# Turning sums over states on TensorE in two halves of 64 channels: a selective-scan block on one Trainium2 core

## The chip, the cores and the metric

The kernel runs on one core of a Trainium2 chip. The metric is device time in microseconds (us) of one execution. The kernel before took 2935.89 us (median of two runs, 2935.25 and 2936.52). The profile shown here is of one further execution of the same kernel, which took 2932.42 us, of which 2930.6 us are the span of its instructions. All times of engines, spacings and waits below are of that execution.

## What is computed

The input is x of 8 x 2048 x 512. A layer norm is followed by a selective scan (state space model with 16 states per channel), added back to x; a second layer norm is followed by a matmul with int8 quantised rows, added back as well. The part that the change touches is the sum over states and the skip term:

```python
deltaA = jnp.exp(jnp.einsum('bld,dn->bldn', delta, A))
deltaB_u = jnp.einsum('bld,bln,bld->bldn', delta, Bm, x)
def step(h, inp):
    dA_t, dBu_t, C_t = inp
    h = dA_t * h + dBu_t
    y = jnp.einsum('bdn,bn->bd', h, C_t)
    return (h, y)
...
y = ys.transpose(1, 0, 2) + x * D
...
x = x + _L0_attn_ref(_layernorm(x, axis=-1), ...)
x = x + _L0_ffn_ref(_layernorm(x, axis=-1), ...)
```

## The kernel before

**Tiling.** The 16384 rows are cut into 32 chunks of 512 time steps; four consecutive chunks are one sequence. In a chunk, the scan runs with channels on the partitions and time along the free axis. The 512 channels are four blocks d of 128, the 512 steps four blocks i of 128. One pair (state n, block d) is a unit; a chunk has 16 x 4 = 64 units, called slots, and there are 2048 units u in all.

**One slot.** ScalarE makes da = exp(delta * A) (`exp_unit`, L673). ScalarE also scales x by B for one block i of a coming state (`bt_piece`, L689). TensorE turns that to channels by time, 4 transposes of 128 x 128 into one PSUM bank pb (`b_pe`, L712). For the states 1, 4, 9, 13 (`DIAG_STATES`) it multiplies by a diagonal matrix of B instead (L703; every fp32 matmul that is no transpose runs as two passes, so 8 matmuls in the trace). VectorE runs the scan over 512 steps (`scan`, L721). Once per state, GpSimd multiplies the four finished blocks of h by C (`c_mult`, L749). TensorE turns hc back to time by channels and sums over states in PSUM in the same step: `y_pe` (L763) is 4 transposes of 128 x 128 for one time block i, into the bank y_i, with `start` only on the first of 16 states. `skip_pe` (L778) adds x * D to the same bank, 4 matmuls (8 passes) with `diag_d`, in the slots `SKIP_AT` = 45, 47, 49 and 51. The last state of the last chunk is turned in `finish` (L799).

**Order.** All instructions are kept in program order on each engine. The main loop goes through the units u and issues, in this order: `c_mult` (when d = 0), `exp_unit`, `bt_piece`, `b_pe(u + 2)`, `scan(u)`, `y_pe(u - 11)`, and then the steps that two tables place in this slot. `PREP_AT` holds the preparation of the next chunk (layer norm, transposes, projections), `POST_AT` (`LATE_AT` for the last two) the second half of the previous chunk: residual add, layer norm, quantisation, the int8 matmul and the store. So TensorE runs two units ahead of VectorE's scan, and the turn of hc runs 11 units behind. The last `y_pe` of a chunk for i = 0, 1, 2, 3 come in slots 7, 8, 9, 10 of the next chunk; the residual adds that read them (L546, VectorE) in slots 8, 10, 12, 13; the first `y_pe` of the next chunk, which write the same banks, in slots 11, 12, 13, 14.

**PSUM.** Eight banks: four for y (tags y0 to y3), three for pb (one pool, `bufs=3`), one for all else (`misc`).

Of the kernel before, what the change touches and what calls it, by code (L numbers as in the profile page):

```python
# [9 lines left out]
F32 = mybir.dt.float32  # L10
# [4 lines left out]
ALU = mybir.AluOpType  # L15
AX = mybir.AxisListType

P = 128
T = 512
LN_EPS = 1e-05  # L20
Q_EPS = 1e-06
# [23 lines left out]

POST_AT = dict(
    load=(0, 6),
    residual=(8, 10, 12, 13),
    stats=(15, 18, 20, 22),
    aggregate=(16, 19, 21, 23),  # L50
    rstd=23,
# [13 lines left out]

LATE_AT = dict(
    load=(0, 6),
    residual=(8, 10, 12, 13),
    stats=(15, 18, 20, 22),
    aggregate=(16, 19, 21, 23),  # L70
    rstd=23,
# [19 lines left out]
def kernel(  # L91
# [13 lines left out]
    nc = tc.nc  # L105

    B, L, DM = x.shape
    N = a_log.shape[1]
# [3 lines left out]
    ND = DM // P  # L112
# [16 lines left out]
    small = ctx.enter_context(tc.tile_pool(name="small", bufs=6))  # L129
    dram = ctx.enter_context(tc.tile_pool(name="dram", bufs=2, space=bass.MemoryType.DRAM))  # L130
    diagd = ctx.enter_context(tc.tile_pool(name="diagd", bufs=1, space=bass.MemoryType.DRAM))
    ps_y = ctx.enter_context(tc.tile_pool(name="ps_y", bufs=1, space=bass.MemoryType.PSUM))
# [3 lines left out]
    pin = tc.keep_in_program_order  # L136
# [15 lines left out]
    ident = const.tile([P, P], F32, name="ident")  # L152
# [31 lines left out]
    diag_d = const.tile([P, ND, P], F32, name="diag_d")  # L184
# [33 lines left out]
    xn_t, delta, b_t = {}, {}, {}  # L218
# [3 lines left out]
    das, pbs, bts, hs, hcs, ys = {}, {}, {}, {}, {}, {}  # L222
# [158 lines left out]
    def prep_first(second):  # L381
# [3 lines left out]
        mv = small.tile([P, NT, 2], F32, tag=f"mv{NT}", name="mv_0")  # L385
# [9 lines left out]
        pts, pps = {}, {}  # L395
# [49 lines left out]
        def dt(i):  # L445
            for d in range(ND):
                if i == 0:
                    pps[d] = ps_y.tile([P, T], F32, tag=f"y{d}", name=f"pdt_0_{d}")
                pin(
                    nc.tensor.matmul(  # L450
                        pps[d][:, ts(i, P)],
                        lhsT=dtproj_sb[:, ts(d, P)],
                        rhs=xp[:, ts(i, P)],
                        start=True,
                        stop=True,
                    )
                )
# [71 lines left out]
        pin(nc.sync.dma_start(out=bias_b, in_=bias.partition_broadcast(P)))  # L529
        zero_diagonals(1)  # L530

    def post(k):

        key = f"f{k}"
# [7 lines left out]
        def x1_of(i):  # L542
            return x1[k, i // 2][:, i % 2, :]

        def residual(i):
            pin(nc.vector.tensor_tensor(x1_of(i), ys.pop((k, i)), x1_of(i), ALU.add))  # L546

        def norm(i):
            if i == 0:
# [201 lines left out]

    def y_pe(s, i):

        if s < 0 or s >= LAST - 1:
            return
        k, n = divmod(s, N)
        if n == 0:
            y = ps_y.tile([P, DM], F32, tag=f"y{i}", name=f"y_{k}_{i}")
            ys[k, i] = y
        y = ys[k, i]  # L760
        for d in range(ND):
            pin(
                nc.tensor.matmul(  # L763
                    y[:, ts(d, P)],
                    lhsT=hcs[s][:, d, ts(i, P)],
                    rhs=ident,
                    is_transpose=True,
                    start=(n == 0 and d == 0),
                    stop=(n == N - 1 and d == ND - 1),
                    skip_group_check=True,  # L770
                )
            )

    def skip_pe(k, i):

        for d in range(ND):
            pin(
                nc.tensor.matmul(  # L778
                    ys[k, i][:, ts(d, P)],
                    lhsT=xn_t[k][:, d, ts(i, P)],  # L780
                    rhs=diag_d[:, d, :],
                    start=False,
                    stop=False,
                    skip_group_check=True,
                )
            )

    def finish():


        k, s = NCHUNK - 1, LAST - 1
        h = hs.pop(s)
        hc = work.tile([P, ND, T], F32, tag="hc", bufs=3, name=f"hc_{k}_{N - 1}")
        c = cts[s // 2][:, (N - 1) % 2, :]
        for d in range(ND):
            pin(nc.vector.tensor_tensor(hc[:, d, :], h[:, d, :], c, ALU.mult))
            for i in range(NT):
                pin(
                    nc.tensor.matmul(  # L799
                        ys[k, i][:, ts(d, P)],  # L800
                        lhsT=hc[:, d, ts(i, P)],
                        rhs=ident,
                        is_transpose=True,
                        start=False,
                        stop=(d == ND - 1),
                        skip_group_check=True,
                    )
                )
        mv = small.tile([P, NT, 2], F32, tag=f"mv{NT}", name="mv_last")
        am = small.tile([P, NT], F32, tag="am", name="am_last")  # L810
        xs = small.tile([P, NT], F32, tag="xs", name="xs_last")
        rs = small.tile([P, NT], F32, tag="rs", name="rs_last")
        ve = small.tile([P, NT], F32, tag="ve", name="ve_last")
        rstd = small.tile([P, NT], F32, tag="rstd", name="rstd_last")
        nmr = small.tile([P, NT], F32, tag="nmr", name="nmr_last")

        z_all = work.tile([P, NT, DM], F32, tag="z", bufs=1, name="z_last")

        def x1_of(i):
            return x1[k, i // 2][:, i % 2, :]  # L820

        def measure(i):
            one = slice(i, i + 1)
            t = x1_of(i)
            pin(nc.vector.tensor_tensor(t, ys.pop((k, i)), t, ALU.add))
            st = small.tile([P, 6], F32, tag="st", name=f"st_last_{i}")
            pin(nc.vector.bn_stats(st, t))
            pin(nc.vector.bn_aggr(mv[:, i, :], st))
            pin(nc.vector.tensor_scalar(ve[:, one], mv[:, i, 1:2], LN_EPS, None, ALU.add))
            pin(nc.gpsimd.tensor_tensor(rstd[:, one], ve[:, one], nhalf[:, one], ALU.pow))  # L830

        def norm(i):
            one = slice(i, i + 1)
            pin(
                nc.vector.tensor_scalar(
                    nmr[:, one], mv[:, i, 0:1], -1.0, rstd[:, one], ALU.mult, ALU.mult
                )
            )
            pin(
                nc.scalar.activation(  # L840
                    z_all[:, i, :], x1_of(i), AF.Identity, bias=nmr[:, one], scale=rstd[:, one]
                )
            )

        def quantise(i):
            one = slice(i, i + 1)
            z = z_all[:, i, :]
            pin(
                nc.vector.tensor_reduce(
                    am[:, one], z, AX.X, ALU.max, apply_absolute_value=True  # L850
                )
            )
            pin(
                nc.vector.tensor_scalar(
                    xs[:, one], am[:, one], Q_EPS, 1.0 / 127.0, ALU.max, ALU.mult
                )
            )
            pin(nc.vector.reciprocal(rs[:, one], xs[:, one]))
            pin(nc.scalar.activation(z, z, AF.Copy, bias=ROUND, scale=rs[:, one]))
            pin(nc.gpsimd.tensor_tensor(x1_of(i), x1_of(i), bias_b, ALU.add))  # L860
            pz = ps_b.tile([P, T], F32, tag="b", name=f"pz_last_{i}")
            for d in range(ND):
                pin(nc.tensor.transpose(pz[:, ts(d, P)], z[:, ts(d, P)], ident))
            qt = work.tile([P, ND, P], BF16, tag="qT", name=f"qT_last_{i}")
            pin(
                nc.scalar.activation(
                    qt, pz.rearrange("p (d t) -> p d t", t=P), AF.Copy, bias=-ROUND
                )
            )
            po = ps_y.tile([P, T], F32, tag=f"y{i}", name=f"po_last_{i}")  # L870
            for d in range(ND):
                pin(
                    nc.tensor.matmul(
                        po, lhsT=qt[:, d, :], rhs=wq_sb[:, d, :], start=(d == 0), stop=(d == ND - 1)
                    )
                )
            return po

        def output(i, po):
            o = z_all[:, i, :]  # L880
            pin(
                nc.vector.scalar_tensor_tensor(
                    o, po, xs[:, i : i + 1], ws_b, ALU.mult, ALU.mult
                )
            )
            adder = nc.vector if i == NT - 1 else nc.gpsimd
            pin(adder.tensor_tensor(o, o, x1_of(i), ALU.add))
            pin(nc.sync.dma_start(out=of[ds(k * T + i * P, P), :], in_=o))

        pos = {}  # L890
        measure(0)
        measure(1)
        norm(0)
        measure(2)
        norm(1)
        pos[0] = quantise(0)
        measure(3)
        norm(2)
        pos[1] = quantise(1)
        norm(3)  # L900
        pos[2] = quantise(2)
        output(0, pos[0])
        pos[3] = quantise(3)
        for i in range(1, NT):
            output(i, pos[i])
# [93 lines left out]
```

## Time and profile before

| | |
|---|---|
| Median of two runs | 2935.89 us |
| The profiled execution, its span | 2932.42 us, 2930.6 us |
| TensorE clock granted | 0.997 of full, over the span |
| First scan starts, last scan starts | 29.4 us, 2901.6 us |
| DMA | 276.46 MB, mean 94 GB/s; largest queue 30.5% of 16 engines' span |
| GpSimd, hc (L749) | 511 x 4566 ns |
| ScalarE, exp (L673) and x * B (L689) | 2048 x 714 ns and 1532 x 712 ns |
| VectorE, residual add (L546) | 124 x 665 ns |

How to read it: PE stands for TensorE's matmuls and PEld for its weight loads, which run beside the matmuls; DVE is VectorE, ACT ScalarE, POOL GpSimd. A transpose is a matmul whose loaded weight is the data (`lhsT`) and whose moving operand is the identity. The duration of a PE row is from start to end of one matmul, and matmuls are pipelined: the rate is read from the distance of starts. In a row of the timeline that holds several instructions (x4), this distance is (length of the row - duration of one) / (count - 1).

### The profile page before, as it was taken

The page shows a single profiled execution, that of the slowest core. Times are in us where ns is not written, and L with a number is a line of the kernel's source. Part 1 is how long each engine was busy: PE and PEld are TensorE (multiplying, and loading weights), DVE is VectorE, ACT ScalarE, POOL GpSimd, SP SyncE. Part 2 cuts the span into 40 slices and gives each one's busy share as a digit, 9 for nine tenths or more (in the row PEclk, how much of TensorE's full clock was granted, in tenths as well). Part 3 has the DMA queues.
Part 4 walks back from the last instruction along what each step waited for, and adds up shares of the span by engine and source line. Part 5 has one row for each costly group of instructions (what it writes and reads, how often), then busy time and mean ns, then how long its engine had stood idle before and what let it go on. Part 6 is the DMA issues. An engine that isn't in the chain of part 4 may idle for free.

```text
span 2930.6 us, 57694 instructions
## 1 busy us (share of the span) xinstructions
PE 2771.6 (95%) x22132; PEld 2461.9 (84%) x22226; DVE 2875.5 (98%) x3077; ACT 2785.3 (95%) x4477; POOL 2791.0 (95%) x1335
## 2 busy tenths in 40 slices
PE   8999999999999999999999999999999999999987
PEld 6888888888888888888888888888888888888886
DVE  6999999999999999999999999999999999999998
ACT  7999999999999999999999999999999999999994
POOL 6899999999999999999999999999999999999997
PEclk9999999999999999999999999999999999999999
DMA  4232332322333323323233332233232232323221
GB/s 139 84 102 72 96 109 95 109 77 88 98 106 98 97 68 106 107 92 107 80 86 103 96 107 81 84 105 99 98 102 77 91 109 95 109 77 88 85 90 62
DMA packets 179989, 276.46 MB, mean 94 GB/s; under 512 B 79169, under 2 KB 79681, under 8 KB 179713
## 3 DMA queue, kind: packets, MB, share of 16 engines
q1 hardware_dynamic: 177520, 272.41, 30.5%
q8 instruction: 174, 2.85, 0.4%
q14 instruction: 103, 0.84, 0.1%
q10 hardware_dynamic: 2192, 0.36, 0.1%
HBM read 235.77 MB, written 36.96 MB: 93 GB/s over the span
## 4 chain that ended last, share of the span: by engine, by line
PE 48%; ACT 30%; DVE 12%; issue 6%; POOL 3%; DMA 1%; ACTq 0%; DVEq 0%; SPq 0%
PE y L763 13%; ACT da L673 12%; PE pb L712 11%; PE pb L703 10%; ACT bT L689 9%; DVE h L721 8%; PE pxp L294 4%; PE po L611 3%; POOL hc L749 3%; PE y L778 2%; PE pdt L333 2%; ACT delta L343 2%; ACT z L552 1%; ACT L673 1%; ACT L343 1%
## 5 line engine op out<-in xcount | busy, mean ns | idle before, releaser
L749 POOL TENSOR_TENSOR hc<-h,c 128x2048 f32<-128x2048 f32 x511 | 2330.9, 4566 | 26.8 <-DVE mv_f L232 11.5
L721 DVE TENSOR_TENSOR_SCAN h<-da,state,pb 128x512 f32<-128x512 f32 x1536 | 1868.7, 1258 | 8.7 <-PE pb L703 3.4
L673 ACT ACTIVATE da<-delta,a_neg 128x512 f32<-128x512 f32 x2048 | 1417.0, 714 | 6.4 <-DVE h L721 5.9
L763 PE MATMUL y<-ident,hc 128*128 128x128 f32 x8176 | 1226.4, 273 | 0.3 <-POOL hc L749 0.3
L689 ACT ACTIVATE bT<-x,BT 128x512 f32<-128x512 f32 x1532 | 1090.4, 712 | 0.0
L712 PE MATMUL pb<-ident,bT 128*128 128x128 f32 x6128 | 948.6, 277 | 83.5 <-DVE h L721 64.2
L712 PEld LDWEIGHTS pb<-ident,bT 128*128 128x128 f32 x6128 | 705.3, 141 | 315.1 <-DVE h L721 132.1
L763 PEld LDWEIGHTS y<-ident,hc 128*128 128x128 f32 x8176 | 957.3, 141 | 1.3 <-POOL hc L749 0.5
L721 DVE TENSOR_TENSOR_SCAN h<-da,pb 128x512 f32<-128x512 f32 x512 | 593.7, 1200 | 17.8 <-PE pb L712 12.2
L703 PE MATMUL pb<-dg,x 128*128 128x128 f32 x4128 | 552.3, 277 | 24.3 <-DVE h L721 21.7
L703 PEld LDWEIGHTS pb<-dg,x 128*128 128x128 f32 x4128 | 506.3, 192 | 59.0 <-DVE h L721 37.1
L564 POOL TENSOR_TENSOR x<-x,bias_b 128x1024 f32<-128x1024 f32 x62 | 147.5, 2379 | 2.5
L632 POOL TENSOR_TENSOR z<-z,x 128x1024 f32<-128x1024 f32 x62 | 147.5, 2379 | 0.0
L333 PE MATMUL pdt<-xp,dtproj_sb 128*128 128x512 f32 x248 | 130.1, 606 | 17.8 <-ACT delta L343 17.8
L778 PE MATMUL y<-diag_d,xnT 128*128 128x128 f32 x1024 | 135.2, 275 | 0.0
L611 PE MATMUL po<-wq_sb,qT 128*128 128x512 bf16 x403 | 122.3, 379 | 8.3 <-ACT qT L600 3.2
L294 PE MATMUL pxp<-xnT,xproj_sb 128*96 128x512 f32 x248 | 126.7, 592 | 0.0
L778 PEld LDWEIGHTS y<-diag_d,xnT 128*128 128x128 f32 x1024 | 124.4, 192 | 0.0
L343 ACT ACTIVATE delta<-pdt,dtb_sb 128x512 f32<-128x512 f32 x124 | 85.0, 685 | 37.2 <-PE pdt L333 36.8
L288 ACT COPY xnT<-pxn 128x512 f32<-128x512 f32 x124 | 72.6, 585 | 34.0 <-PE pxn L282 31.9
L270 ACT ACTIVATE x<-x,nmr_a,rstd_a 128x512 f32<-128x512 f32 x124 | 100.8, 813 | 0.0
L552 ACT ACTIVATE z<-x,nmr_f,rstd_f 128x512 f32<-128x512 f32 x124 | 99.4, 803 | 0.0
(100 smaller groups left out, 1660.0 us busy)
## 6 DMA issues: line engine op xcount, KB each, us to landing
c<-bc SPq DMA_DIRECT2D x256, 512.0 KB, 4.0
x<-in_x_dram SPq DMA_DIRECT2D x64, 512.0 KB, 5.2
dg<-dg SPq DMA_DIRECT2D x127, 256.0 KB, 4.7
x<-in_x_dram SPq DMA_DIRECT2D x31, 1024.0 KB, 7.9
out_dram<-z SPq DMA_DIRECT2D x62, 512.0 KB, 4.8
dg<-zeros SPq DMA_DIRECT2D x8, 256.0 KB, 6.0
dg<-BT SPq DMA_DIRECT2D x128, 2.0 KB, 3.7
x<-in_x_dram SPq DMA_DIRECT2D x4, 256.0 KB, 3.9
```

The costliest lines, as they stand in the source:

```text
L294: nc.tensor.matmul(st["pp"][:E], lhsT=xproj_sb[:, d, :], rhs=xn_t[k][:, d, :], start=(d == 0), stop=(d == ND - 1),)
L333: nc.tensor.matmul(pd, lhsT=dtproj_sb[:, ts(d, P)], rhs=xp, start=True, stop=True)
L343: nc.scalar.activation(delta[k][:, d, :], st.pop(("pd", d)), AF.Softplus, bias=dtb_sb[:, d : d + 1])
L611: nc.tensor.matmul(po, lhsT=qt[:, d, :], rhs=wq_sb[:, d, :], start=(d == 0), stop=(d == ND - 1))
L673: pin(nc.scalar.activation(t, delta[k][:, d, :], AF.Exp, scale=a_neg[:, d, n : n + 1]))
L689: nc.scalar.activation(bts[s][:, i, :], xn[k][:, i, :], AF.Copy, scale=b_t[k][:, i, n : n + 1])
L703: nc.tensor.matmul(pb[:, ts(i, P)], lhsT=xn[k][:, i, ts(d, P)], rhs=bts[s][:, i, :], start=True, stop=True,)
L712: pin(nc.tensor.transpose(pb[:, ts(i, P)], bts[s][:, i, ts(d, P)], ident))
L721: nc.vector.tensor_tensor_scan(hs[s][:, d, :], das.pop(u), pbs.pop(u), 0.0 if k % CPB == 0 else state[n][:, d : d + 1], ALU.mult, ALU.add,)
L749: pin(nc.gpsimd.tensor_tensor(hc, h, c.unsqueeze(1).to_broadcast([P, ND, T]), ALU.mult))
L763: nc.tensor.matmul(y[:, ts(d, P)], lhsT=hcs[s][:, d, ts(i, P)], rhs=ident, is_transpose=True, start=(n == 0 and d == 0), stop=(n == N - 1 ...
L778: nc.tensor.matmul(ys[k, i][:, ts(d, P)], lhsT=xn_t[k][:, d, ts(i, P)], rhs=diag_d[:, d, :], start=False, stop=False, skip_group_check=True,)
```

## The change

Each transpose of `y_pe`, each transpose of `finish` and each matmul of `skip_pe` becomes two, one for channels 0 to 63 and one for channels 64 to 127 of the block, one after the other. A half has 64 contracted rows (partitions 0 to 63 or 64 to 127 of the data and of the identity or `diag_d`), still 128 loaded columns, and 64 moving columns instead of 128. In the built program these have a tile size of 64 x 128 at row 0 or row 64 of the array; all other matmuls keep 128 x 128. Two time blocks share a tile of two banks: bank 0 has the lower halves of both blocks, bank 1 the upper halves, so the halves of one transpose go to different banks. `start` is set on the first half in each bank alone.

The residual add reads its 512 columns as 8 runs of 64 from the two banks, and the first residual add moves from slot 8 to slot 9, since block 1's last sum (slot 8) now lies in the same tile; `POST_AT` and `LATE_AT` change alike. The banks used are eight as before. The instructions of VectorE, ScalarE, GpSimd and SyncE are the same in number, and in order but for that add.

```diff
-    residual=(8, 10, 12, 13),
+    residual=(9, 10, 12, 13),
...
+    def split(t):
+        return t.rearrange("p (d h c) -> p d h c", h=2, c=HALF)
...
         def residual(i):
-            pin(nc.vector.tensor_tensor(x1_of(i), ys.pop((k, i)), x1_of(i), ALU.add))
+            t = split(x1_of(i))
+            pin(nc.vector.tensor_tensor(t, y_of(k, i), t, ALU.add))
...
     def y_pe(s, i):
...
-        if n == 0:
-            y = ps_y.tile([P, DM], F32, tag=f"y{i}", name=f"y_{k}_{i}")
-            ys[k, i] = y
-        y = ys[k, i]
+        if n == 0 and i % 2 == 0:
+            ys[k, i // 2] = ps_y.tile(
+                [P, 2, 2, ND, HALF], F32, tag=f"y{i // 2}", name=f"y_{k}_{i // 2}"
+            )
         for d in range(ND):
+            y_halves(k, i, d, hcs[s], first=(n == 0 and i % 2 == 0 and d == 0))
+
+    def y_halves(k, i, d, hc, first=False, last=False):
+        for half in range(2):
+            rows = ds(half * HALF, HALF)
             pin(
                 nc.tensor.matmul(
-                    y[:, ts(d, P)],
-                    lhsT=hcs[s][:, d, ts(i, P)],
-                    rhs=ident,
+                    ys[k, i // 2][:, half, i % 2, d, :],
+                    lhsT=hc[rows, d, ts(i, P)],
+                    rhs=ident[rows, rows],
                     is_transpose=True,
-                    start=(n == 0 and d == 0),
-                    stop=(n == N - 1 and d == ND - 1),
+                    start=first,
+                    stop=last,
                     skip_group_check=True,
                 )
             )
+    def y_of(k, i):
+        return ys[k, i // 2][:, :, i % 2, :, :].rearrange("p h d c -> p d h c")
...
     def skip_pe(k, i):
         for d in range(ND):
-            pin(
-                nc.tensor.matmul(
-                    ys[k, i][:, ts(d, P)],
-                    lhsT=xn_t[k][:, d, ts(i, P)],
-                    rhs=diag_d[:, d, :],
...
+            for half in range(2):
+                rows = ds(half * HALF, HALF)
+                pin(
+                    nc.tensor.matmul(
+                        ys[k, i // 2][:, half, i % 2, d, :],
+                        lhsT=xn_t[k][rows, d, ts(i, P)],
+                        rhs=diag_d[rows, d, rows],
...
```

`finish` calls `y_halves` for its 16 transposes, and the pieces of chunk 0 and of the last chunk that borrow the y banks (`dt` in `prep_first`, `po_last`) take them in pairs.

## The prediction, on record before the changed kernel ran

> **What bounds the kernel now.** I read the page's busy times, then its groups by line, the waits, the timeline (for the distance of matmul starts), and last the busy times of three stretches: before the first scan, between first and last scan, and after.
>
> ```profile
> PE 2771.6 (95%) x22132; PEld 2461.9 (84%) x22226; DVE 2875.5 (98%) x3077; ACT 2785.3 (95%) x4477; POOL 2791.0 (95%) x1335
> ...
> L721 DVE TENSOR_TENSOR_SCAN h<-da,state,pb 128x512 f32<-128x512 f32 x1536 | 1868.7, 1258 | 8.7 <-PE pb L703 3.4
> L763 PE MATMUL y<-ident,hc 128*128 128x128 f32 x8176 | 1226.4, 273 | 0.3 <-POOL hc L749 0.3
> ```
> ```profile
> 29.40:2901.60 2872.20, 2737.55 (x21925) 2435.22 (x22019) 2843.60 (x3001) 2760.86 (x4441) 2768.38 (x1302) 1.00 0.31 94
> ```
> The second fence gives the length and then PE, PEld, DVE, ACT, POOL, clock and DMA. VectorE is busy 2843.6 of 2872.2 us: 28.6 us are left, 0.9 per chunk. It is the bound, and nothing done to TensorE can gain more than about that. The waits say how much of it is TensorE's doing, and where TensorE itself stops for VectorE:
>
> ```profile
> PE pb L712 <- DVE h L721: 64.2, 139, 2.0
> ...
> PE pb L703 <- DVE h L721: 21.7, 49, 1.6
> ...
> DVE h L721 <- PE pb L712: 13.2, 15, 2.2
> ...
> DVE h L721 <- PE pb L703: 5.5, 9, 0.9
> ```
> VectorE waits 13.2 + 5.5 us for pb, some 21 us with the small rows (y 0.8, po 1.0, pdl 0.4). TensorE waits 64.2 + 21.7 = 86 us for a free pb, 2.8 per chunk: its whole reserve against VectorE. It is uneven. After the last x * D of a chunk (1536.24) the timeline of PE has one gap, 0.29 us, in 10 us.
>
> ```profile
> 1536.24 1.06 PE L778 MATMUL y<-diag_d,xnT 128*128 128x128 f32 x8
> ```
> ```profile
> 61.82 0.60 PE L763 MATMUL y<-ident,hc 128*128 128x128 f32 x4
> 62.25 0.50 PE L314 MATMUL pbt<-ident,xp 96*128 96x96 f32 x4
> 62.59 0.60 PE L712 MATMUL pb<-ident,bT 128*128 128x128 f32 x4
> ```
> ```profile
> 85.08 0.42 PEld L712 LDWEIGHTS pb<-ident,bT 128*128 128x128 f32 x4
> 85.08 0.66 PE L712 MATMUL pb<-ident,bT 128*128 128x128 f32 x4
> ```
> Starts of y transposes are (0.60 - 0.273) / 3 = 0.109 us apart, those of x * D (1.06 - 0.275) / 7 = 0.112. With 96 moving columns and the same 128 loaded columns, L314 takes (62.59 - 62.25) / 4 = 0.085. So a transpose is limited by its moving columns, in proportion (96/128 of 0.109 is 0.082), and a load of 128 columns needs 0.085 at most. After a wait it shows less: the four loads at 85.08 have 0.42 - 0.141 = 0.279 between first and last; with two steps of 0.109 that leaves 0.06 for the first. For x * D the step of 0.112 is 0.003 above that of the moving columns; I read it as load-bound.
>
> **The change, part by part.** TensorE's stream is now 8176 x 0.109 = 891 us for y, 1024 x 0.112 = 115 for x * D, and the rest (6128 x 0.109 and 4128 x 0.112 for pb, 496 x 0.429 for the 512-column fp32 passes, 496 x 0.216 for po, 1488 x 0.109 and 124 x 0.085 for the other transposes) 1620, in all some 2626 us, 82 per chunk of 89.8 (2872.2 / 32).
>
> *y in halves.* 16,352 loads and matmuls stand for 8176. A half moves 64 columns: 0.055 by proportion; its load costs 0.06. What no row shows is whether the two halves, in other rows of the array and other banks, run side by side. Bounds: a pair takes 0.06 if they do and 0.12 (two loads) if they don't, against 0.109. The nearest row for two streams in the array at once is PEld beside PE: busy 84% and 95% of the same span, a load passing through all rows under a running matmul. Two halves share neither rows, partitions nor banks, which is less than those two share; I take 0.06. Then y costs 8176 x 0.06 = 491 us, 400 less, 0.2 per slot.
>
> *x * D in halves.* 2048 passes for 1024. Side by side a pair costs one load, 0.112: nothing changes. One after another it is 229 us, 115 more, 0.9 in each of four slots. I take 0.
>
> *Changing between 128 and 64 rows.* Twice per slot, 4096 times. The rows above show a change to 96 rows and back without a gap (62.25 is 61.82 + 4 x 0.109), so the lower bound is 0. The upper one is a matmul finished before the next load begins: 0.273 - 0.109 = 0.164, and an uncovered load of 0.06, so 0.22. I take 0, by that row. The Trainium skill, page TensorEngine Tiling (Array Packing), Key Properties, speaks against it: going from one tiling mode to another drains TensorE. No row here has another mode; by that rule at the upper bound the sum would be the second rival's.
>
> *Issue.* PE's queue gets some 18,400 instructions more (22132 matmuls become 31,350, with a load each). At 85.08 a load, a matmul and a load start within 0.06 us, so 0.02 each is possible; y needs 0.06 / 4 = 0.015 at best. Up to 0.027 each, y would merely cost what it does now (16 x 0.027 = 0.436).
>
> *The residual add.* 128 VectorE instructions read 8 runs of 64 from two banks. Nothing at least; the nearest dearer row is the add with a permuted operand in the first chunk (L520, 690 ns against 663 of L356): 0.027 x 128 = 3.5 us, all on the bound. I take 3. The first add, moved past one scan, costs nothing: its norm statistics come in slot 15.
>
> *The waits on y's banks.* The next chunk's first y of block 2 (slot 13) now waits for the add of block 3, which follows scan 13; before, it waited for that of block 2 in slot 12. TensorE stands for up to 1.17 + 0.58 = 1.75 us (one scan and one add by distance of starts); queued behind it are pb 16, the transposes of x and all later ones. VectorE holds pb 14 and 15 then, two scans and a statistic, 2.9 us; TensorE needs y, pb and a transpose group, 1.3, so I cost it at nothing. With that cover gone it is at most 31 x 1.75 = 54 us. In slot 11 the wait is for the add of slot 10, shorter.
>
> *Sum.* TensorE's 400 us are off the path. VectorE loses the waits for TensorE, 21 us, and pays 3: 2932.4 - 21 + 3 = 2914. The two runs' median is 3.5 above the profiled execution: **2918 us**. Next late are ScalarE and GpSimd (2761 and 2768 busy of 2872), whose work is untouched. The case's own range is 2895 (all 28.6 gained, and some idling that overlapping rows hide) to 2945 (half of the row-change bound paid, which the 0.2 per slot just covers).
>
> **The rivals.** *One after another.* If loads of the two halves follow each other, y gets 16,352 x 0.06 = 981 us, 90 more (0.045 per slot), and x * D 0.9 more in slots 45, 47, 49, 51. For: every load here starts after the one before it. Against: those are all loads of the full 128 rows. Of the 3.6 us in x * D's stretch some 0.6 meet idle time (PE waits for VectorE before slot 50), 3.0 push VectorE; y adds about 0.8 where TensorE has no reserve. 31 x 3.8 = 118: **3053 us**. It decides from a pair above some 0.115.
>
> *The array drains at each change of row size.* Against 0.2 saved per slot stands twice the price, so it decides from 0.1. At 0.164 TensorE has 0.13 more per slot, 8.3 per chunk; its reserve of 2.8 taken off, 5.5 x 31 = 170: **3105 us**. At 0.22 it is (15.4 - 2.8) x 31 = 390, 3325; with the halves also one after another, more. For: an array whose upper rows have to take no sum from the lower ones is set otherwise. Against: the 96-row transposes.
>
> *Issue-bound, no change.* TensorE issues no faster than 0.027 each: y takes 0.436 per slot as before, **2939 us** with the residual adds' 3. For: no row here has more than three instructions in 0.06. Against: the rate has never been asked for in this trace.
>
> The page TensorE: Matmul & The Clock Gate, Part 3, has matmuls in different row groups start some 4 ns apart; no run here shows it yet, and by it alone the forecast stands.
>
> **How the numbers follow.** Forecast 0.46; drain 0.25; one after another 0.20; issue-bound 0.07; another mishap 0.02. About 2% (2877 to 2995) is what a measurement of this kernel tells from no change. Faster by more than that needs over 57 us, twice VectorE's idle time: 0.02. Within: 0.45 of the forecast, 0.07 issue-bound, 0.02 of the small drains: 0.54. Slower: 0.44. The likeliest case has 2895 to 2945; the range to hold 8 in 10 goes up through the first rival and the drain at 0.164, to 3140, and leaves out the dearer drains (0.13) and a little below 2895.
>
> **What would show it.** Right: y's pairs start 0.06 us apart or less on average, the wait of VectorE for pb nearly gone, TensorE's waits for VectorE well over 86 us, the adds near 0.69. Wrong: a step of 0.06 from half to half (one after another); a gap before the first half of each group and after its last (drain); VectorE's waits for pb in the hundreds of us; y in slot 13 waiting and scan 16 late behind it.

## The result, and the profile after

The changed kernel takes 3064.11 us (median of 3062.40 and 3065.83), 1.0437 times the kernel before, 95% interval 1.0392 to 1.0482: slower by 4.4%, where 0.6% faster was forecast. The profiled execution took 3062.40 us, its span is 3060.6.

First the page's busy times and the chain that ended last, and two of the groups by line (L777 is y's line now, L728 the scan's):

```profile
PE 2922.3 (95%) x31442; PEld 2249.9 (74%) x31442; DVE 2908.2 (95%) x3077; ACT 2789.6 (91%) x4477; POOL 2791.7 (91%) x1335
...
PE 73%; DVE 19%; issue 5%; ACT 2%; DMA 0%; DVEq 0%; ACTq 0%
...
L728 DVE TENSOR_TENSOR_SCAN h<-da,state,pb 128x512 f32<-128x512 f32 x1536 | 1880.9, 1261 | 70.5 <-PE pb L719 41.4
...
L777 PE MATMUL y<-ident,hc 64*128 64x64 f32 x16384 | 947.8, 235 | 46.2 <-DVE x L553 44.4
```

The bound has moved: TensorE now holds 73% of the chain, and the scan's idle time went from 8.7 to 70.5 us. The busy share of PE, 95% as before, tells nothing of it. The waits, longest first, say more:

```profile
PEld y L777 <- issue: 242.6, 1433, 2.0
...
DVE h L728 <- PE pb L719: 64.2, 155, 1.1
...
PE y L777 <- DVE x L553: 44.4, 31, 1.8
...
DVE h L728 <- PE pb L710: 30.2, 113, 1.1
```

VectorE's waits for pb grew from 13.2 and 5.5 us to 64.2 and 30.2, and TensorE's wait for the residual adds, which the prediction had costed at nothing, is 44.4 us in 31 pieces. The longest row, 242.6 us in which y's loads stand idle behind "issue", is new too. What it is, the timeline of PE and of its loads shows:

```profile
201.53 0.66 PE L719 MATMUL pb<-ident,bT 128*128 128x128 f32 x4
202.12 0.47 PE L777 MATMUL y<-ident,hc 64*128 64x64 f32 x8
202.51 0.66 PE L719 MATMUL pb<-ident,bT 128*128 128x128 f32 x4
```
```profile
201.53 0.42 PEld L719 LDWEIGHTS pb<-ident,bT 128*128 128x128 f32 x4
202.12 0.33 PEld L777 LDWEIGHTS y<-ident,hc 64*128 64x128 f32 x8 [0.17 <-issue]
202.51 0.20 PEld L719 LDWEIGHTS pb<-ident,bT 128*128 128x128 f32 x2
```

From pb to pb it is 202.51 - 201.53 = 0.98 us, against 8 x 0.109 = 0.87 before. In it, four pb transposes are 0.44 and eight halves are four pairs of 0.06, 0.24 (the trace has the two loads of a pair 0.003 to 0.007 us apart, and the two matmuls 0.003 to 0.005). That leaves 0.30 for the two changes of row size, **0.15 each**. The single starts agree: after a full matmul the first load of a half waits 0.201 us from that matmul's start, and its own load, 0.057, is not hidden, where the normal step is 0.109; 0.201 + 0.057 - 0.109 = 0.149. On the way back the load starts 0.151 after the last pair, the step would have been 0.060: 0.151 + 0.057 - 0.060 = 0.148. Before a half the 0.20 stands at 98 of 100 changes outside the half-clock pieces; on the way back 0.15 stands at 83 of 100 and 0.20, behind x * D, at 6; at most of the others the row of the next load shows a wait. PE's busy time cannot show it, since a matmul's row of 0.27 us covers the 0.2 us in which nothing starts.

Per slot, then, 0.20 us are saved on y and 0.30 paid for the changes. By the distance of scan starts (mean of chunks 1 to 29) the changed kernel loses 4.06 us per chunk. Most of it is at the scans of slots 7, 22, 25, 30, 32, 36, 38, 54 and 55, which come 0.25 to 0.64 us late each.

The stretch behind the last scan takes 33.30 us instead of 29.00, at a mean granted clock of 0.55 instead of 0.86.

### The profile page after: what moved, and what is told of

The parts are those of the page before. It is cut to its first block, busy times and chain, and to the rows that moved or that the text cites. A ratio compares the mean times of both kernels' runs of the same rounds, so it can differ in the third digit from the quotient of the medians.

```text
span 3060.6 us, 76316 instructions
## 1 busy us (share of the span) xinstructions
PE 2922.3 (95%) x31442; PEld 2249.9 (74%) x31442; DVE 2908.2 (95%) x3077; ACT 2789.6 (91%) x4477; POOL 2791.7 (91%) x1335
## 4 chain that ended last, share of the span: by engine, by line
PE 73%; DVE 19%; issue 5%; ACT 2%; DMA 0%; DVEq 0%; ACTq 0%
PE y L777 19%; PE pb L719 18%; PE pb L710 16%; DVE h L728 13%; PE pdt L334 4%; PE pxp L295 4%; PE y L798 3%; PE po L618 3%; DVE x L553 2%; PE pz L601 2%; DVE x L357 2%; PE pxn L283 1%; PE pdl L352 1%; DVE z L627 1%; ACT delta L344 1%
## 5 line engine op out<-in xcount | busy, mean ns | idle before, releaser
L728 DVE TENSOR_TENSOR_SCAN h<-da,state,pb 128x512 f32<-128x512 f32 x1536 | 1880.9, 1261 | 70.5 <-PE pb L719 41.4
L719 PE MATMUL pb<-ident,bT 128*128 128x128 f32 x6128 | 976.2, 282 | 53.5 <-DVE h L728 47.1
L777 PE MATMUL y<-ident,hc 64*128 64x64 f32 x16384 | 947.8, 235 | 46.2 <-DVE x L553 44.4
L777 PEld LDWEIGHTS y<-ident,hc 64*128 64x128 f32 x16384 | 668.6, 138 | 366.9 <-issue 242.6
L719 PEld LDWEIGHTS pb<-ident,bT 128*128 128x128 f32 x6128 | 678.0, 141 | 272.7 <-issue 137.0
L728 DVE TENSOR_TENSOR_SCAN h<-da,pb 128x512 f32<-128x512 f32 x512 | 597.7, 1202 | 39.2 <-PE pb L719 22.8
L710 PE MATMUL pb<-dg,x 128*128 128x128 f32 x4128 | 577.5, 283 | 3.0 <-DVE h L728 1.6
L710 PEld LDWEIGHTS pb<-dg,x 128*128 128x128 f32 x4128 | 507.5, 192 | 43.3 <-issue 14.8
L753 POOL COPY state<-h 128x4 f32<-128x4 f32 x384 | 73.9, 192 | 86.2 <-DVE h L728 42.3
L295 PE MATMUL pxp<-xnT,xproj_sb 128*96 128x512 f32 x248 | 136.2, 631 | 0.0
L798 PE MATMUL y<-diag_d,xnT 64*128 64x64 f32 x2048 | 135.5, 272 | 0.0
L798 PEld LDWEIGHTS y<-diag_d,xnT 64*128 64x128 f32 x2048 | 125.4, 189 | 0.2 <-issue 0.2
```

The lines of the kernel that those rows point to most:

```text
L295: nc.tensor.matmul(st["pp"][:E], lhsT=xproj_sb[:, d, :], rhs=xn_t[k][:, d, :], start=(d == 0), stop=(d == ND - 1),)
L710: nc.tensor.matmul(pb[:, ts(i, P)], lhsT=xn[k][:, i, ts(d, P)], rhs=bts[s][:, i, :], start=True, stop=True,)
L719: pin(nc.tensor.transpose(pb[:, ts(i, P)], bts[s][:, i, ts(d, P)], ident))
L728: nc.vector.tensor_tensor_scan(hs[s][:, d, :], das.pop(u), pbs.pop(u), 0.0 if k % CPB == 0 else state[n][:, d : d + 1], ALU.mult, ALU.add,)
L777: nc.tensor.matmul(ys[k, i // 2][:, half, i % 2, d, :], lhsT=hc[rows, d, ts(i, P)], rhs=ident[rows, rows], is_transpose=True, start=first, ...
L798: nc.tensor.matmul(ys[k, i // 2][:, half, i % 2, d, :], lhsT=xn_t[k][rows, d, ts(i, P)], rhs=diag_d[rows, d, rows], start=False, stop=Fals ...
```

## The experiments

Three theories stood against each other. A: each change of row size costs TensorE 0.15 us, and that is nearly all of the loss. B: the loss is the new wait on y's shared banks. C: TensorE is short of instructions, as the "issue" row seems to say. "Before" is 2934.65 to 2935.08 us in these runs. Where no interval is given, the kernel was run once.

**The wait on y's banks taken away** (e_resid).

```diff
-    residual=(9, 10, 12, 13),
+    residual=(9, 10, 11, 12),
```


> The changed kernel with the four residual adds in slots 9, 10, 11, 12 instead of 9, 10, 12, 13, so that the next chunk's first y of block 2 (slot 13) finds its bank read before scan 13. Theory A (every change between 128 and 64 rows costs TensorE some 0.15 us; the bank waits are minor): in the changed kernel's trace the wait of y for the adds is 44.4 us in 31 pieces; without it TensorE would still wait for scan 13 before pb 16, so about half is real, 3064 - 20 = 3040 us, and the switch gaps stay. Theory B (the loss is the new wait on y's banks, which holds up all pb behind it): some 3064 - 90 = 2970 us. Theory C (TensorE is short of instructions, 18,600 more of them): 3064, unchanged.

Measured: 3051.72 us, ratio 1.0399 (1.0383 to 1.0414). TensorE's matmuls no longer wait for the adds, and its loads, which waited 49.7 us, hardly do:

```profile
PEld y L777 <- DVE x L553: 5.0, 30, 0.2
```

The time fell by 12 us by the medians, though the two intervals overlap. Part of the wait only moved on: the row `PE pb L710 <- DVE h L728` went from 1.6 to 23.3 us. B is out as the main cause, since it foresaw 2970 (and A 3040): 44.4 us of waiting were worth some 12.

**Half as many changes** (e_group2): the turns of two time blocks in one go.

```diff
-        y_pe(*divmod(u - 11, ND))
+        if (u - 11) % 2 == 1:
+            for w in (u - 12, u - 11):
+                y_pe(*divmod(w, ND))
...
-SKIP_AT = (45, 47, 49, 51)
+SKIP_AT = (46, 48, 50, 52)
```


> The changed kernel with the turns of two time blocks issued together, in every second slot (blocks 0 and 1 in the slot of block 1, 2 and 3 in that of block 3); x * D moved to slots 46, 48, 50, 52 so that it stays beside a turn. Same instructions, half as many changes of row size (about 2050 for 4096). Theory A: TensorE saves 2048 x 0.149 = 305 us, 9.5 per chunk, which takes it some 3 us per chunk below the kernel before: 2910 to 2940 us. Theory B: the wait of slot 13 goes as well, since block 2 now comes in slot 14: 2970. Theory C: the same number of instructions, 3064.

Measured: 2974.72 us, ratio 1.0139 (1.0122 to 1.0156). With the same instructions, 89 us of the 128 are back. C is out, which foresaw no change. Between A and B this run does not decide, since the wait of slot 13 goes with it: the time is 35 us above the upper end of what A foresaw, and 5 from B's 2970. By the distance of scan starts, slot by slot (mean of chunks 1 to 29), nearly all of what it is slower than the kernel before is in one place: the scan of slot 55, right after that of slot 54, is on average 1.06 us late. The timeline of VectorE there:

```profile
1467.11 2.42 DVE L728 TENSOR_TENSOR_SCAN h<-da,state,pb 128x512 f32<-128x512 f32 x2
1470.54 3.62 DVE L728 TENSOR_TENSOR_SCAN h<-da,state,pb 128x512 f32<-128x512 f32 x3 [1.01 <-PE pb L710]
```

TensorE had two turns and x * D in each of slots 50 and 52, beside the state with two passes per matmul (L710) and a quantisation group: the work had become less, but it came in lumps.

**A quarter of the changes** (e_group4): all four time blocks of a state in one go.

```diff
-        y_pe(*divmod(u - 11, ND))
+        if (u - 11) % ND == ND - 1:
+            for i in range(NT):
+                y_pe((u - 11) // ND, i)
...
-    residual=(9, 10, 12, 13),
+    residual=(10, 11, 12, 13),
...
-SKIP_AT = (45, 47, 49, 51)
+SKIP_AT = (38, 42, 46, 50)
```


> The changed kernel with the turns of all four time blocks of a state issued together, in the slot of block 3; adds in slots 10, 11, 12, 13, x * D in slots 38, 42, 46, 50. A quarter of the changes of row size (about 1024). Theory A: TensorE 14.3 us per chunk below the changed kernel, 7.7 below the kernel before; VectorE is the bound again, 2900 to 2925 us, unless the bursts of 1.3 us make pb late. Theory B: 2970. Theory C: 3064.

Measured: 3015.21 us, ratio 1.0274 (1.0259 to 1.0290), 90 us above what A foresaw and worse than two blocks. TensorE's work did shrink: it waits 228.9 us for VectorE in its largest wait, against 64.2 in the kernel before. Two things take the gain. A lump is 1.2 us long and VectorE, two units behind, waits for pb. And after some stretches in which TensorE idles, its clock is cut. Two neighbouring stretches, with length and then PE, PEld, DVE, ACT, POOL, clock, DMA share and GB/s:

```profile
1450.00:1455.80 5.80, 4.00 (x44) 2.73 (x39) 5.80 (x6) 5.62 (x9) 5.80 (x2) 1.00 0.49 55
1455.80:1459.20 3.40, 3.40 (x38) 2.60 (x37) 1.48 (x2) 2.00 (x3) 1.85 (x1) 0.50 0.66 227
```

PE is busy 4.00 of 5.80 us, then gets half its clock for 3.4 us, and VectorE does 1.48 us of work in that time. The profile has 17 such pieces here, 91 us together (head and tail included), against 4 and 20 us in the kernel before. Chunk by chunk the trace tells what is the clock's share. A chunk at full clock already takes 2.82 us more than in the kernel before (0.47 in the first chunk of a sequence); the seven of chunks 1 to 29 that have a piece take 12 us more, all together, than their likes without one. So of the 76 us lost in these chunks some 64 are lost at full clock.

**Not by turns** (e_noturn): four lower halves, then four upper ones.

```diff
-        for d in range(ND):
-            y_halves(k, i, d, hcs[s], first=(n == 0 and i % 2 == 0 and d == 0))
+        for half in range(2):
+            for d in range(ND):
+                y_halves(k, i, d, hcs[s], first=(n == 0 and i % 2 == 0 and d == 0), halves=(half,))
```


> The changed kernel with the halves of a turn not by turns: the four lower halves of a time block first, then its four upper halves. Same instructions and the same two changes of row size per slot. Theory A with halves side by side only when neighbours differ in rows: a group takes 7 or 8 steps of 0.06 instead of 4, 0.18 to 0.24 more per slot, all on the path: 3064 + 31 x 64 x (0.18 to 0.24) = 3420 to 3540 us. If each half of the array ran on its own whatever the order, or if the halves were not side by side at all, nothing changes: 3064.

Measured: 3076.27 us, 12 more than the changed kernel. The group is hardly longer:

```profile
1002.45 0.48 PE L778 MATMUL y<-ident,hc 64*128 64x64 f32 x8
1002.86 0.33 PE L719 MATMUL pb<-ident,bT 128*128 128x128 f32 x1
```

From the first half to the next full load it is 0.41 us, against 0.39 by turns. The 3420 us, which need the halves to start strictly in the order issued, are refuted. The rows do not name the half, but the eight starts come in pairs 0.014 to 0.018 us apart, as they come in pairs by turns: I read each pair as a lower and an upper half, so that the fifth instruction starts beside the first. The two row halves then run as two streams, whatever the order of issue. The Trainium skill, TensorE: Matmul & The Clock Gate, Part 3, has it otherwise: matmuls start and end strictly in program order. For matmuls in different rows this run, so read, contradicts it.

**The price of the changes by itself** (e_zero64, with e_zero128 as its control): the kernel before with one added transpose of zeros behind each turn, which leaves the result as it is.

```diff
+        pin(
+            nc.tensor.matmul(
+                y[:, :64],
+                lhsT=zero_sb[:64],
+                rhs=ident[:64, :64],
+                is_transpose=True,
+                start=False,
+                stop=False,
+                skip_group_check=True,
+            )
+        )
```


> The kernel before with one more transpose behind each turn (2044 in all): 64 rows of a block of zeros, added to 64 columns of y, so nothing of the result changes. It adds two changes of row size per slot and 0.06 us of work, and no halves. Theory A (0.149 us per change): TensorE gets 0.298 + 0.06 = 0.36 more per slot, 22.9 per chunk; its reserve of 2.8 taken off, 20 x 31 = 620 us more, about 3555 us, with gaps of about 0.2 and 0.15 at the changes. If the changes cost nothing and the loss came from what the halves bring (shared banks, more instructions): 0.06 per slot, 3.8 per chunk, some 30 us more, 2965.

> The control: the kernel before with one more transpose of 128 rows of zeros behind each turn. 0.109 us per slot, 7.0 per chunk, no change of row size. Theory A: (7.0 - 2.8) x 31 = 130 us more, about 3065 us; the difference to the 64-row one is then 490 us, the price of 4088 changes less 0.05 of work each pair. If an added transpose disturbs the order in some other way, both come out alike.

Measured: 3435.01 us with 64 rows, 3023.97 with 128 (where the added transpose has `y[:, :P]`, all of `zero_sb` and of `ident`). The smaller transpose costs 411 us more than the larger. PE's timeline, first 64 rows, then 128:

```profile
203.07 0.60 PE L765 MATMUL y<-ident,hc 128*128 128x128 f32 x4
203.60 0.27 PE L776 MATMUL y<-ident,zero_sb 64*128 64x64 f32 x1
203.80 0.44 PE L714 MATMUL pb<-ident,bT 128*128 128x128 f32 x2
```
```profile
203.19 0.60 PE L765 MATMUL y<-ident,hc 128*128 128x128 f32 x4
203.62 0.27 PE L776 MATMUL y<-ident,zero_sb 128*128 128x128 f32 x1
203.73 0.49 PE L714 MATMUL pb<-ident,bT 128*128 128x128 f32 x3
```

From the turn to the next pb it is 0.73 us against 0.54, and the first load after a change (0.06) is to be added. Here y's banks are not shared, no turn is in halves, and of the changed kernel's 18,622 added instructions there are 4183, the same number in both kernels. So the loss follows the changes. In all these kernels the moving columns change together with the row size; that columns alone cost nothing of the kind is shown for 96 of them only (L314, without a gap). Both kernels came out below what was expected (3555 and 3065); their difference, 490 by theory, is 411: by it a change costs (411 / 2044 + 0.05) / 2 = 0.126 us at the end of the kernel, less than the 0.149 in the rows; that part of it falls where TensorE waits anyway would explain this and was not measured.

**Two blocks per group, x * D elsewhere** (e_group2_early, e_group2_spread, e_group2_spread2, e_group2_last). All four are e_group2 with only `SKIP_AT` moved, and with the last chunk's int8 results in banks of their own:

```diff
-            if i % 2 == 0:
-                st["po"] = ps_y.tile([P, 2, T], F32, tag=f"y{i // 2}", name=f"po_last_{i // 2}")
-            po = st["po"][:, i % 2, :]
+            if i == 2:
+                po = misc(f"po_last_{i}")
+            else:
+                tag = f"y{i % 2}" if i < 2 else "y0"
+                po = ps_y.tile([P, 2, T], F32, tag=tag, name=f"po_last_{i}")[:, 0, :]
```


> Two time blocks per group as before, with x * D in slots 40, 42, 44, 46, where TensorE waits for VectorE, instead of 46 to 52, and with the last chunk's outputs of the int8 matmul in banks of their own. Theory A with bursts: the scan of slot 54 was 1.06 us late in each chunk because turns, x * D and a quantisation group meet in slots 50 and 52; this goes: 2974.7 - 31 x 1.06 = 2942, and the tail's 4 us: 2938, so about the kernel before (2920 to 2945). If the remaining loss is not from that meeting: 2970.

> Two time blocks per group, with x * D in slots 12, 24, 42, 44, each where TensorE waits for VectorE. In the run with slots 40 to 46 the granted clock fell to half for 3.4 us nine times (61 us in all), seven of them in the middle of the kernel around slots 24 to 28, every fourth chunk. Theory A with the clock: x * D in slot 24 fills that stretch, those pieces go and with them some 2 us each, 2942 - 14 = 2928; with the halves' saving that is just below the kernel before. If the half-clock pieces cost nothing, or the added work at 24 makes the scans of 31 to 33 late: 2942 or more.

> As the one before with x * D in slots 12, 14, 42, 44: less work before slots 31 to 33, and the stretch around slot 24 stays thin. Theory A with the clock: the half-clock pieces stay, 2935 to 2945. If they cost nothing: like the one before or 5 us better.

> Two time blocks per group, x * D in slots 12, 24, 46, 48. With x * D in slots 42 and 44 the scan after slot 43 came 0.3 us late in each chunk, since the turn, x * D and a transpose of delta meet in slot 42; in slots 46 and 48 it did not. Theory: 2940.5 - 31 x 0.3 = 2931, the level of the kernel before, less if the two x * D at 46 and 48 leave slots 53 to 55 as they are. If the half-clock pieces take it back: 2940 again.

| x * D in slots | us | ratio to before (95%) | half-clock pieces of the profiled execution |
|---|---|---|---|
| 46, 48, 50, 52 (e_group2) | 2974.72 | 1.0139 (1.0122 to 1.0156) | 6, 53 us |
| 40, 42, 44, 46 (early) | 2942.52 | 1.0029 (1.0019 to 1.0038) | 9, 61 us |
| 12, 24, 42, 44 (spread) | 2940.52 | 1.0025 (1.0014 to 1.0036) | 6, 44 us |
| 12, 14, 42, 44 (spread2) | 2992.61 | 1.0198 (1.0184 to 1.0212) | 20, 108 us |
| 12, 24, 46, 48 (last) | 2937.57 | 1.0010 (1.0001 to 1.0019) | 3, 42 us |

The first row to the second: 32 us by the medians, as expected. The scan of slot 55 is no longer late; 0.15 and 0.28 us per chunk came back at the scans of slots 32 and 44. Spread against spread2 differs in one x * D, from slot 24 to 14, and in 52 us; that was not expected (2935 to 2945). The same stretch of both, 24 first:

```profile
883.00:889.80 6.80, 6.80 (x74) 5.83 (x73) 6.80 (x7) 6.77 (x11) 6.80 (x3) 1.00 0.37 119
889.80:893.20 3.40, 3.17 (x47) 2.57 (x46) 3.40 (x4) 3.40 (x6) 3.24 (x4) 1.00 0.00 1
```
```profile
883.00:889.80 6.80, 5.12 (x56) 3.65 (x55) 6.80 (x6) 6.77 (x11) 6.80 (x3) 1.00 0.49 84
889.80:893.20 3.40, 3.40 (x25) 2.32 (x24) 1.44 (x2) 2.11 (x4) 2.57 (x3) 0.50 0.85 220
```

Where PE was busy 5.12 of 6.80 us, the clock halves for the next 3.4 us, and VectorE works 1.44 of them; x * D in slot 24 keeps the clock there. In spread2 the scan of slot 32 is on average 1.4 us late per chunk. But the clock is only about half of that: 16 of chunks 1 to 29 have such a piece, and in the other 13, at full clock, the scans of slots 27 to 34 still come 0.9 us later than in spread. What else differs is that TensorE waits longer for ScalarE's delta, 31 times in both. The row first in spread, then in spread2:

```profile
PE pdt L334 <- ACT delta L344: 19.1, 31, 1.5
```
```profile
PE pdt L334 <- ACT delta L344: 51.9, 31, 1.7
```

That this wait makes the scans late in the other 13 was not tested apart. The nine pieces of early belong to an execution of 2949.52 us, granted 0.990 of the clock; its four executions granted 0.993 took 2939.60 to 2940.27. For spread 2928 was foreseen if the pieces go, and for last 2931; both came out above. So the place of TensorE's work can cost more than the work itself, and no version with halves got below the kernel before.

**x * D moved, whole transposes** (e_before_spread, e_before_last): the kernel before with `SKIP_AT` = 12, 25, 42, 44 and 12, 25, 45, 47.

> The kernel before, whole transposes, with x * D in slots 12, 25, 42, 44: no halves and no change of row size. It tells what moving x * D alone brings. VectorE waits some 0.3 us per chunk in slots 53 to 55 behind x * D and the quantisation; that goes, 9 us, and 0.4 or more may come back in slots 31 to 33: 2925 to 2940. If the halves in groups are what gains, this stays above them.

> The kernel before with whole transposes and x * D in slots 12, 25, 45, 47. Against slots 12, 25, 42, 44 (2930.75) the 0.11 us at slot 43 goes, 3 us: 2927. If halves in groups have an advantage of their own, the other kernel of this call is below it by 3 us per chunk of TensorE time as far as VectorE can use it, 10 us at most.

Measured: 2930.75 us, ratio 0.9984 (0.9975 to 0.9993), and 2931.74, 0.9988 (0.9979 to 0.9997). Both are just faster than the kernel before and than every version with halves. The second was expected 3 us below the first and is not; the two can't be told apart. VectorE's largest wait for pb is 10.9 us in the first:

```profile
DVE h L721 <- PE pb L712: 10.9, 23, 1.4
```

## Why the prediction was wrong

- *What bounds the kernel.* Right for the kernel before. VectorE left 28.6 us; the best of all versions here gained 4, so no run shows that the 21 us of waits were to be had.
- *y in halves.* Right in mechanism and size: a pair takes 0.06 us, the two halves side by side, 8 starts in 0.24. The first rival, one half after the other, did not occur; that its 3053 us lies close to the result is chance.
- *x * D in halves.* Right: its pairs follow each other at 0.112 us, as the whole passes did.
- *Changing between 128 and 64 rows.* **This is the step that failed.** It was put at 0 by the row of the 96-row transposes; it is 0.149 us, within the bounds of 0 and 0.22 and near the 0.164 of a matmul that has to finish first. 4096 x 0.149 = 610 us against 400 saved: 210 more for TensorE, less its reserve of 86, makes 124; measured are 128. That the two lie so close is in part luck: the changed kernel still has 48.7 us of waits for a free pb, so the reserve is not all used, and the 128 hold the wait for the adds and the tail too. The row chosen did not show the thing priced: 96 active rows in a tile of 128 are no other tiling of the array. The same sum stood in the second rival (3105 at 0.164); it had been given a chance of 0.25. The Trainium skill's rule, TensorEngine Tiling (Array Packing), Key Properties, that going to another tiling mode drains TensorE, was right; it has no figure, and the trace gives one.
- *Issue.* Right that it does not limit: two loads and two matmuls start within 0.06 us. The 242.6 us under "issue" are the pauses at the changes of row size, as e_group2 (120 us in the same row's place with half the changes) and e_zero64 show.
- *The residual add.* 668 ns for 665 per add: 0.003 x 128 = 0.4 us, not 3. Eight runs of 64 from two banks cost nothing that matters.
- *The wait in slot 13.* Costed at nothing because VectorE has two scans in hand there. TensorE did stand 44.4 us, and its removal was worth some 12. The cover held at slot 13 itself: the scans of slots 13 to 16 are not late. But the scan of slot 22 is 0.42 us late per chunk, and 0.12 with the wait taken away; over 31 chunks that is 9 of the 12.
- *The tail.* Not priced; 4.3 us, at a lower granted clock.

## What to carry to other kernels

Price the border between two ways of using an engine, not only the work inside each: here the work got 0.20 us per slot cheaper and the two borders cost 0.30. If the tiling of the array must change, put as much as possible between two changes, but not in lumps longer than the lead that the next engine has. And before taking work from an engine, look at which engine ends each stretch: with VectorE at 98%, nothing done to TensorE could gain more than 1%, while every loss of TensorE in the slots without reserve was a loss of the kernel.

## What the runs showed of the hardware that was not expected

- Transposes in the lower and the upper 64 rows run side by side as two streams, loads too, and by the reading above not in the order of issue (0.41 us for a group of eight by halves, 0.39 by turns, from its first start to the next full load).
- A change of row size costs 0.149 us in either direction by the rows, for fp32 transposes; 0.126 by the two kernels with transposes of zeros.
- The granted clock halves in pieces of 3.41 us (4 of them, head and tail included, in the kernel before; 17 and 20 in e_group4 and e_group2_spread2). In each of these traces, and in that of e_group2_early, all pieces start whole multiples of 3.413 us apart. In e_group4, e_group2_early and e_group2_spread2, chunks 1 to 29, PE is busy for 0.45 to 0.51 of the 3.41 us before a piece. In e_group2_early only the first chunk of each sequence comes so low there (0.51), and the others stay at 0.72 or more; so the pieces come every fourth chunk. But the busy time alone does not decide. Here is a stretch before a piece of e_group2_early, then one of e_group2_spread2 that no piece follows:

```profile
424.30:427.71 3.41, 1.73 (x22) 1.28 (x22) 3.41 (x4) 3.38 (x5) 3.41 (x3) 1.00 0.80 49
```
```profile
521.16:524.58 3.42, 1.75 (x13) 0.91 (x10) 3.13 (x3) 3.05 (x4) 3.42 (x3) 1.00 0.68 49
```

What else decides stays open.
